# A transformer stack on one core: both halves of a tick's scores issued together in the first block

## The chip, the core and the metric

The kernel runs on one core of a Trainium2 chip. The metric is the time of one execution on the device in microseconds; lower is better. A core has a matrix engine (TensorE, in the profile PE, with its weight loads as PEld), VectorE (DVE), ScalarE (ACT), GpSimd (POOL) and SyncE (SP), which here only issues DMAs. Each engine works through its own list of instructions in the order in which the program wrote them; semaphores make one engine wait for another. TensorE writes its results into PSUM, a memory of eight banks of 128 partitions x 512 floats, and VectorE and ScalarE read them there.

## The reference, cut to what matters

A batch of 32 samples of 128 tokens x 144 channels goes through four layers in a row: an attention block with an MLP (L0), a rotation in a 64-dimensional subspace (L1), a second attention block with an MLP (L2), and an attention block with four experts of which each token uses two (L3). The change concerns the attention of L0:

```
q, k = ln(q, g_q), ln(k, g_k)                                    # 16 heads of 9 channels
attn = softmax(einsum('bhqd,bhkd->bhqk', q, k) * 9 ** -0.5)
o    = einsum('bhqk,bhkd->bhqd', attn, v)
x    = x + g_msa * (o @ w_proj + b_proj)
x    = x + g_mlp * (gelu(ln_mod(x) @ w1 + b1) @ w2 + b2)
```

For L1 the kernel also needs the Q of a QR decomposition of a 144 x 64 matrix and, for each sample, the exponential of a 64 x 64 skew matrix. Both depend on the weights and the condition alone, and the kernel computes them beside the first block.

## The kernel before, in words

**Tiling.** One sample is one tile: 128 tokens on the partitions. Four samples make a group, and some products (MLP, L2's and L3's projections) run for a group at once. The kernel is one unrolled software pipeline whose step is called a *tick*. In each tick three samples are in the attention part: `s0` gets its scores, for the maxima of the softmax; `s1`, one sample older, gets its scores again with the maxima already subtracted, for the weights; `s2`, older by one more, has its values weighed and projected. The ticks of the first block are 0 to 31, those of the second begin at tick `first[1]` = 39 (B + GAP, GAP = 7), those of the third at 71. The order of the emissions is written out by hand: the main loop (L1281 to L1325) calls the attention steps, and `fill(tick, gap)` puts whatever was planned with `put` for that place (L1168 to L1263). The program's order is each engine's order; nothing is reordered afterwards.

**A tick of the first block, in order** (L1289 to L1325). Gap "a": a QR column is broadcast (`ps_qr`, L324; ScalarE squares and copies it, GpSimd takes a root), then the transposes `ps_hT_m` of a finished sample and their two ScalarE copies hM_m and hR_m (L663). "t": two more pieces of QR on VectorE, which end in the update of `at` (L356). `scores(s0, s1, 0)`. Gap "stats": every fourth tick from tick 10 on the first part of `mlp1` (three products with `hR_m` into three banks `ps_h`, L673). `weigh(s2)`: 32 small products into `ps_o`, and ScalarE's copy `on` (L882). "b": a second linear layer `ps_f`, the values `ps_v`, the transposes `ps_hT_a`, a piece of the matrix exponential (`ps_odd`, `ps_sq` and others), the rest of that mlp1 with its three gelus. "den": the next QR column, and VectorE's statistics of the layer norms. `sums(s2)` (L889 to L894): two transposes back into `ps_o`, from which VectorE takes the reciprocals rd and spreads them to rdx. `scores(s0, s1, 1)`. "c": the projection to q and k of a later sample and its transposes (`ps_qk`, `ps_qkT`, with ScalarE's qT, kT and qksq). `divide_T` (L901), pieces of QR, `divide` (oT, L906). "d": other parts of the MLP. `largest_T` and `largest` (L808, L813): the maxima are transposed and added to q as q2, which s0's weights of the next tick need. "z": a piece of the matrix exponential, among others. `project_out`: `ps_pj` (L927), res_a (L916), and the sum into x, which GpSimd does early in the next tick.

**scores(s, w, n)** (L819) does one half of the heads. For s it fills two banks `ps_s` with four products of K = 32 and 256 columns, for w two banks `ps_w` with eight products of K = 32 and 128 columns; the rows of the two differ, so that the four 32-row parts of the array are all used. An fp32 product shows as two records in the profile. VectorE then takes the maxima of each `ps_s` bank (L854, two reductions), and ScalarE the exponentials of each `ps_w` bank (L861, two activations) into a tile `pr`.

**PSUM.** Pool `ps_o` is one bank, which `weigh`, `sums` and `divide_T` of a sample use in turn. Pool `ps_m` is the other seven, given out by `bank()` (L78). A bank goes back to the pool behind the last instruction that reads it, in the order of the program; the first product into it then waits for that reader:

```
ps_o = ctx.enter_context(tc.tile_pool(name="ps_o", bufs=1, space=PSUM))
ps_m = ctx.enter_context(tc.tile_pool(name="ps_m", bufs=7, space=PSUM))
```

Of the kernel before, what the change touches and what calls it, by code (L numbers as in the profile page):

```python
# [8 lines left out]
F32 = mybir.dt.float32  # L9
# [8 lines left out]
B, T, C = 32, 128, 144  # L18
# [47 lines left out]
def tile_kernel(ctx: ExitStack, tc: tile.TileContext, a: dict, out: bass.AP):  # L66
# [7 lines left out]
    ps_o = ctx.enter_context(tc.tile_pool(name="ps_o", bufs=1, space=PSUM))  # L74
# [3 lines left out]
    def bank(shape, name):  # L78

        n = 1  # L80
        for s in shape[1:]:
            n *= s
        t = ps_m.tile([128, 512], F32, tag="m", name=name)
        v = t[: shape[0], :n]
        if len(shape) == 3:
            v = v.rearrange("p (a b) -> p a b", b=shape[2])
        elif len(shape) == 4:
            v = v.rearrange("p (a b c) -> p a b c", b=shape[2], c=shape[3])
        return v
# [161 lines left out]
    def rows4(i):  # L251
        return slice(32 * i, 32 * i + 32)
# [44 lines left out]
    def load_gates(layer, g, n):  # L297

        t = work.tile([128, G, C], F32, tag=f"gates{n}", name=f"gates_{layer}_{g}_{n}")
        nc.sync.dma_start(  # L300
            t.rearrange("p b c -> p (b c)"),
            gates[layer, n, g * G * C : (g + 1) * G * C].partition_broadcast(128),
        )
        return t
# [315 lines left out]
    def of(s):  # L620
        layer, b = divmod(s, B)
        return layer, b, (layer, b // G), b % G
# [182 lines left out]
    def largest_T(s, ot):  # L805

        st[s]["nmT"] = bank([128, T], f"ps_nm_{s}") if ot is None else ot[:, 3 * T : 4 * T]
        nc.tensor.transpose(st[s]["nmT"], st[s].pop("nm"), ident)  # L808
# [7 lines left out]
        )  # L816
        st[s]["q2"] = q2

    def scores(s, w, n):  # L819


        mm = ([], [])
        if s is not None:
            layer, b, g, i = of(s)
            qT, kT = gr[g]["qT"], gr[g]["kT"].rearrange("p (r t) n -> p r t n", t=2)
            cols = slice(i * T, (i + 1) * T)
            ps = [bank([128, 4 * T], f"ps_s_{s}_{n}_{e}") for e in range(2)]
            if n == 0:
                st[s]["nm"] = take_nm()
            for t in range(2):  # L830
                for e in range(2):
                    rows = rows4(2 * n + e)
                    o = ps[e].rearrange("p (r t k) -> p r t k", r=2, t=2)[:, :, t, :]
                    mm[0].append((o, qT[rows, t, cols], kT[rows, :, t, cols]))
        if w is not None:
            layer, b, g, i = of(w)
            kT, q2 = gr[g]["kT"], st[w]["q2"]
            cols = slice(i * T, (i + 1) * T)
            pw = [bank([128, 4 * T], f"ps_w_{w}_{n}_{e}") for e in range(2)]
            for k in range(4):  # L840
                for e in range(2):
                    rows = rows4(2 * (1 - n) + e)
                    mm[1].append((pw[e][:, k * T : (k + 1) * T], kT[rows, k, cols], q2[rows, k % 2, :]))

        order = []
        for t in range(2):
            order += mm[0][2 * t : 2 * t + 2] + mm[1][4 * t : 4 * t + 4]
        for o, x, y in order:
            nc.tensor.matmul(o, x, y, start=True, stop=True)  # L849
        if s is not None:  # L850
            nmv = st[s]["nm"].rearrange("p (q s) -> p q s", s=SLOT)
            for e, view in enumerate(ps):
                at0 = 4 * n + 2 * e
                nc.vector.tensor_reduce(  # L854
                    nmv[:, at0 : at0 + 2, ONE : ONE + 2],
                    view.rearrange("p (r t k) -> p r t k", t=2, k=T), AX.X, ALU.max, negate=True,
                )
        if w is not None:
            pr = work.tile([128, 8, T], F32, tag="pr", name=f"pr_{w}_{n}", bufs=4)
            for e, view in enumerate(pw):  # L860
                nc.scalar.activation(  # L861
                    pr[:, 4 * e : 4 * e + 4, :].rearrange("p s q -> p (s q)"), view, AF.Exp,
                    scale=SCALE,
                )
            st[w]["pr", 1 - n] = pr

    def weigh(s):

        ot = ps_o.tile([128, 512], F32, tag="o", name=f"ps_o_{s}")
        st[s]["ot"] = ot  # L870
        po = ot[:, : 2 * T].rearrange("p (t q) -> p t q", t=2)
        v, prs = st[s].pop("v"), [st[s].pop(("pr", n)) for n in range(2)]
        for t in range(2):
            for r in range(2):
                for j in ROWS:
                    nc.tensor.matmul(  # L876
                        po[rows4(j), t, :], v[:, 4 * j + 2 * t + r, :],
                        prs[j // 2][:, 4 * (j % 2) + 2 * r + t, :],
                        start=r == 0, stop=r == 1,
                    )  # L880
        on = work.tile([128, 2, T], F32, tag="on", name=f"on_{s}")
        nc.scalar.copy(on, po)  # L882
        st[s]["on"] = on

    def sums(s):

        po = st[s]["ot"][:, : 2 * T].rearrange("p (t q) -> p t q", t=2)
        for t in range(2):
            nc.tensor.transpose(po[:, t, :], st[s]["on"][:, t, :], ident)  # L889
        den = po.rearrange("p t (s c) -> p t s c", c=SLOT)[:, :, :, ONE]  # L890
        rd = small.tile([128, 2, 8], F32, tag="rd", name=f"rd_{s}")
        nc.vector.reciprocal(rd, den)
        rdx = work.tile([128, 2, 8, SLOT], F32, tag="rdx", name=f"rdx_{s}")
        nc.vector.tensor_copy(rdx, rd.unsqueeze(3).to_broadcast([128, 2, 8, SLOT]))  # L894
        st[s]["rdx"] = rdx

    def divide_T(s):
        po = st[s]["ot"][:, : 2 * T].rearrange("p (t q) -> p t q", t=2)
        rdx = st[s].pop("rdx")
        for t in range(2):  # L900
            nc.tensor.transpose(po[:, t, :], rdx[:, t, :, :].rearrange("p s c -> p (s c)"), ident)  # L901

    def divide(s):
        po = st[s]["ot"][:, : 2 * T].rearrange("p (t q) -> p t q", t=2)
        oT = work.tile([128, 2, T], F32, tag="oT", name=f"oT_{s}")
        nc.vector.tensor_tensor(oT, st[s].pop("on"), po, ALU.mult)  # L906
        st[s]["oT"] = oT
# [254 lines left out]
    GAP = 7  # L1162
    first = (0, B + GAP, 2 * B + GAP)
# [22 lines left out]
    for layer in range(3):  # L1186
        ahead = 5 if layer == 0 else 6
        for n in range(NG):
            g = (layer, n)
            t0 = first[layer] + n * G  # L1190
            for i in range(G):
                s = layer * B + n * G + i
# [75 lines left out]
    def fill(tick, gap):  # L1268
        prepare_qr(tick, gap)
        while (tick, gap) == (last_prep, "d") and late is None:  # L1270
            prepare_qr(tick, gap)
            prepare_expm(tick, gap)

        if gap == ("t" if tick < 0 else "den" if tick < first[1] else "stats") and tick in stats:
            ln_stats(stats.pop(tick))
        for f, args in gaps.pop((tick, gap), ()):
            f(*args)
        prepare_expm(tick, gap)

    last_prep = first[1] - 8  # L1280
    for tick in range(-6, first[2] + B + 14):  # L1281
        s0, s1, s2 = (at_tick.get(tick - k) for k in range(3))
        for layer in range(3):
            for n in range(NG):
                if tick == first[layer] + n * G:
                    gr[layer, n]["ga"] = load_gates(layer, n, 0)
                if tick == first[layer] + n * G + (6 if layer else 9):
                    gr[layer, n]["gm"] = load_gates(layer, n, 1)
        fill(tick, "a")  # L1289
        while sums_later:  # L1290
            sums_later.pop()()
        fill(tick, "e")
        fill(tick, "t")
        scores(s0, s1, 0)
        fill(tick, "stats")
        if s2 is not None:
            weigh(s2)
        fill(tick, "b0")
        fill(tick, "b")
        fill(tick, "den")  # L1300
        if s2 is not None:
            sums(s2)
        fill(tick, "pre1")
        scores(s0, s1, 1)
        fill(tick, "c")
        joined = tick >= first[1]
        if s2 is not None:
            divide_T(s2)
        fill(tick, "y1")
        if s2 is not None and not joined:  # L1310
            divide(s2)
        fill(tick, "y2")
        if not joined:
            fill(tick, "d")
        if s0 is not None:
            largest_T(s0, st[s2]["ot"] if s2 is not None and joined else None)
        if s2 is not None and joined:
            divide(s2)
        if s0 is not None:
            largest(s0)  # L1320
        fill(tick, "z")
        if joined:
            fill(tick, "d")
        if s2 is not None:
            project_out(s2)  # L1325
# [167 lines left out]
```

## Time and profile before

| what | us |
| --- | --- |
| median of 3 timed runs (lowest, highest) | 1423.7 (1420.84, 1427.12) |
| the profiled execution's own time | 1412.95 |
| its span, first to last instruction | 1411.1 |
| TensorE busy in the span | 1333.3 |
| ScalarE busy | 819.2 |
| VectorE busy | 798.3 |
| GpSimd busy | 623.4 |
| first block: first scores of tick 0 to first scores of tick 31 | 40.0 to 440.7 |

The page gives each engine's busy time, then rows of 40 slices of the span in which a digit is the busy share in tenths; the row PEclk, TensorE's granted clock, is 9 in all of them. A line of the waits reads: engine and instruction, what released it, the sum of such waits in us, how often, the longest. A line of the timeline reads: start, duration, engine, line, operation, output and inputs, shapes, how many records are merged in it. TensorE's ends are modelled, so a wait inside a run of products can hide in its busy time; the starts are what to go by.

### The profile page before, as it was taken

The numbers are of one execution on the slowest core, as the hardware profiler recorded it, in microseconds if no ns is written. First come the engines' busy times: TensorE is split into PE (matmuls) and PEld (weight loads), VectorE is DVE, ScalarE is ACT, GpSimd is POOL, SyncE is SP. The second block draws the span as 40 slices with busy tenths as digits, with TensorE's granted clock in tenths as the row PEclk, the third lists the DMA queues.
The fourth block names the chain that finished last, engine by engine and source line by source line (L and its number), as shares of the span: only waits on it lengthen the run. The fifth ranks groups of instructions, "written<-read, shape, count | busy, mean of one in ns | idle before, by whom it ended". The sixth has DMA issues, their size and how long they took to land.

```text
span 1411.1 us, 36544 instructions
## 1 busy us (share of the span) xinstructions
PE 1333.3 (94%) x14530; PEld 976.5 (69%) x14530; DVE 798.3 (57%) x2652; ACT 819.2 (58%) x1912; POOL 623.4 (44%) x1647
## 2 busy tenths in 40 slices
PE   6989898999989988999999999999999999999998
PEld 4667576686766566677767666777776767677765
DVE  5798888877864256565555555544444444343211
ACT  3657767656756445666666666555555555554431
POOL 5567667654643433343333334425252525151522
PEclk9999999999999999999999999999999999999999
DMA  8200000000003100000100000200000000000000
GB/s 221 57 2 19 19 19 2 19 3 20 19 1 117 34 2 18 10 19 10 42 27 18 10 18 11 73 10 18 9 19 9 19 10 18 10 18 2 18 9 9
DMA packets 21612, 34.78 MB, mean 25 GB/s; under 512 B 2176, under 2 KB 12256, under 8 KB 21184
## 3 DMA queue, kind: packets, MB, share of 16 engines
q1 hardware_dynamic: 20848, 31.82, 7.7%
q8 instruction: 117, 1.92, 0.6%
q10 hardware_dynamic: 592, 0.59, 0.2%
q14 instruction: 55, 0.45, 0.1%
HBM read 29.93 MB, written 2.47 MB: 23 GB/s over the span
## 4 chain that ended last, share of the span: by engine, by line
PE 68%; DVE 4%; ACT 2%; issue 1%; POOL 1%; POOLq 0%; DVEq 0%
PE ps_h L673 17%; PE ps_f L953 16%; PE ps_s L849 6%; PE ps_w L849 6%; PE ps_qk L673 5%; PE ps_o L876 5%; PE ps_pj L927 3%; PE ps_v L673 2%; PE ps_o L889 1%; DVE nm L854 1%; PE ps_o L901 1%; PE ps_g L673 1%; DVE oT L906 1%; PE ps_z L985 1%; PE ps_o L808 0%
## 5 line engine op out<-in xcount | busy, mean ns | idle before, releaser
L861 ACT ACTIVATE pr<-ps_w 128x512 f32<-128x512 f32 x384 | 208.5, 596 | 165.4 <-PE ps_w L849 164.7
L854 DVE TENSOR_REDUCE nm<-ps_s 128x4 f32<-128x512 f32 x384 | 246.8, 684 | 82.3 <-PE ps_w L849 68.9
L849 PE MATMUL ps_w<-q,kT 32*128 32x128 f32 x3072 | 236.4, 284 | 0.9 <-ACT hR_m L663 0.6
L849 PE MATMUL ps_s<-kT,qT 32*128 32x256 f32 x1536 | 234.8, 408 | 0.1
L849 PEld LDWEIGHTS ps_w<-q,kT 32*128 32x128 f32 x3072 | 198.6, 187 | 16.1 <-issue 3.6
L947 ACT ACTIVATE hid<-ps_h 128x512 f32<-128x512 f32 (+1 forms) x224 | 119.2, 590 | 119.1 <-PE ps_h L673 119.1
L953 PE MATMUL ps_f<-mlps,hid 128*128 128x144 f32 x1280 | 181.2, 292 | 0.5 <-ACT hid L947 0.5
L953 PEld LDWEIGHTS ps_f<-mlps,hid 128*128 128x128 f32 x1280 | 165.1, 191 | 18.4 <-issue 11.6
L913 POOL TENSOR_TENSOR x_sb<-x_sb,res_a 128x144 f32<-128x144 f32 x96 | 47.0, 489 | 266.8 <-DVE res_a L916 266.7
L1064 DVE SCALAR_TENSOR_TENSOR acc<-ps_f,cw,acc 128x144 f32<-128x144 f32 x128 | 46.9, 367 | 197.6 <-PE ps_f L953 175.8
L849 PEld LDWEIGHTS ps_s<-kT,qT 32*128 32x128 f32 x1536 | 135.0, 186 | 26.8 <-issue 9.2
L673 PE MATMUL ps_h<-hM_m,mlps 128*128 128x512 f32 x304 | 143.8, 606 | 0.0
L876 PE MATMUL ps_o<-pr,vaug 128*32 128x128 f32 x3072 | 104.8, 277 | 0.4 <-issue 0.4
L876 PEld LDWEIGHTS ps_o<-pr,vaug 128*32 128x32 f32 x3072 | 78.7, 110 | 33.8 <-PE ps_w L849 19.0
L673 PEld LDWEIGHTS ps_h<-hM_m,mlps 128*128 128x128 f32 x304 | 53.4, 190 | 66.2 <-issue 64.7
L906 DVE TENSOR_TENSOR oT<-on,ps_o 128x256 f32<-128x256 f32 x96 | 40.0, 417 | 96.3 <-PE ps_o L808 92.9
L953 PEld LDWEIGHTS ps_f<-pair,hid 128*128 128x128 f32 x640 | 82.3, 190 | 9.6 <-issue 8.4
L953 PE MATMUL ps_f<-pair,hid 128*128 128x144 f32 x640 | 86.8, 287 | 0.2 <-ACT hid L947 0.2
L913 POOL TENSOR_TENSOR x_sb<-x_sb,res_m 128x144 f32<-128x144 f32 x64 | 32.8, 512 | 111.4 <-DVE res_m L916 111.2
L634 POOL TENSOR_SCALAR rs_m_a<-mv_m_a 128x2 f32<-128x2 f32 x81 | 15.5, 191 | 142.9 <-DVE mv_m_a L632 115.5
L663 ACT ACTIVATE hM_m<-ps_hT_m,modM 128x128 f32<-128x128 f32 x96 | 44.1, 460 | 58.4 <-PE ps_hT_m L661 58.2
L861 ACT ACT_TABLE_LOAD x55 | 70.6, 1283 | 8.4 <-PE ps_w L849 7.6
(312 smaller groups left out, 2823.2 us busy)
## 6 DMA issues: line engine op xcount, KB each, us to landing
gates<-gates SPq DMA_DIRECT2D x48, 288.0 KB, 3.6
x_sb<-in_x SPq DMA_DIRECT2D x8, 288.0 KB, 10.2
out_x<-x_sb SPq DMA_DIRECT2D x8, 288.0 KB, 2.4
mlps<-in_L_mlp SPq DMA_DIRECT2D x2, 1000.0 KB, 6.3
wt<-in_W SPq DMA_DIRECT2D x6, 320.0 KB, 8.0
pair<-in_L_mlp SPq DMA_DIRECT2D x1, 1872.0 KB, 10.1
mlps<-in_L_mlp SPq DMA_DIRECT2D x1, 1872.0 KB, 7.6
mlps<-in_L_wmod SPq DMA_DIRECT2D x4, 290.0 KB, 6.3
```

The source lines that it names most:

```text
L663: nc.scalar.activation(gr[g][f"{k}_{kind}"][:, i, :], ps[:, k == "hR", :], AF.Identity, bias=m[:, sh, b : b + 1], scale=m[:, sc, b : b + 1],)
L673: nc.tensor.matmul(ps, x, y, start=k == 0, stop=k == 1)
L849: nc.tensor.matmul(o, x, y, start=True, stop=True)
L854: nc.vector.tensor_reduce(nmv[:, at0 : at0 + 2, ONE : ONE + 2], view.rearrange("p (r t k) -> p r t k", t=2, k=T), AX.X, ALU.max, negate=True,)
L861: nc.scalar.activation(pr[:, 4 * e : 4 * e + 4, :].rearrange("p s q -> p (s q)"), view, AF.Exp, scale=SCALE,)
L876: nc.tensor.matmul(po[rows4(j), t, :], v[:, 4 * j + 2 * t + r, :], prs[j // 2][:, 4 * (j % 2) + 2 * r + t, :], start=r == 0, stop=r == 1,)
L906: nc.vector.tensor_tensor(oT, st[s].pop("on"), po, ALU.mult)
L913: nc.gpsimd.tensor_tensor(x_sb[:, b, :], x_sb[:, b, :], t, ALU.add)
L927: nc.tensor.matmul(ps, oT[:, t, :], w[:, t, :], start=t == 0, stop=t == 1)
L947: nc.scalar.activation(hid[:n, i], ps[:n], AF.Gelu_apprx_tanh)
L953: nc.tensor.matmul(ps, hid[:, at0, i, :], w2[:, m, :], start=m == 0, stop=m == NFC - 1)
L1064: nc.vector.scalar_tensor_tensor(acc, ps, w, acc, ALU.mult, ALU.add)
```

## The change

In ticks below `first[1] - GAP` = 32, thus in every tick of the first block that has an s0, the second half of the scores is issued directly behind the first. The two halves then need eight banks at once: seven of `ps_m`, and for the first bank of the first half's weights the one of `ps_o`. The second half's exponentials follow its products at once, in ScalarE's list ahead of `on` and of all of gap "b". The second half's two maxima are kept back as a function and written where the second half stood before, after `sums` and gap "pre1". Later ticks are as they were.

```diff
-    def scores(s, w, n):
+    def scores(s, w, n, at_once=False):
...
-            pw = [bank([128, 4 * T], f"ps_w_{w}_{n}_{e}") for e in range(2)]
+            pw = [
+                ps_o.tile([128, 4 * T], F32, tag="o", name=f"ps_w_{w}_{n}_{e}")
+                if at_once and n == e == 0
+                else bank([128, 4 * T], f"ps_w_{w}_{n}_{e}")
+                for e in range(2)
+            ]
...
-        if s is not None:
+
+        def maxima():
+            if s is None:
+                return
             nmv = st[s]["nm"].rearrange("p (q s) -> p q s", s=SLOT)
...
+        later = at_once and n == 1
+        if not later:
+            maxima()
         if w is not None:
             pr = work.tile([128, 8, T], F32, tag="pr", name=f"pr_{w}_{n}", bufs=4)
...
+        return maxima if later else None
...
-        scores(s0, s1, 0)
+
+        at_once = tick < first[1] - GAP
+        scores(s0, s1, 0, at_once)
+        if at_once:
+            maxima = scores(s0, s1, 1, True)
         fill(tick, "stats")
         if s2 is not None:
             weigh(s2)
...
         fill(tick, "pre1")
-        scores(s0, s1, 1)
+        if at_once:
+            maxima()
+        else:
+            scores(s0, s1, 1)
         fill(tick, "c")
```

## The prediction

> **What bounds the kernel now.** I read the page first, then the busy times by stretch of the first block, then the waits of each engine there, then the timeline of single ticks. "Tick k" is the tick that makes sample k's scores; its start is the first ps_s matmul (L849) of that tick.
>
> ```profile
> span 1411.1 us, 36544 instructions
> ...
> PE 1333.3 (94%) x14530; PEld 976.5 (69%) x14530; DVE 798.3 (57%) x2652; ACT 819.2 (58%) x1912; POOL 623.4 (44%) x1647
> ...
> DVE  5798888877864256565555555544444444343211
> ```
>
> Over the whole span PE is the full engine, but the change touches only ticks 0 to 31, from 40.0 us to about 442 us, and there (slices 2 to 12) VectorE's row stands at 7 to 8. By stretches (ticks 6 to 13, then 18 to 22):
>
> ```profile
> core 0: us, PE busy (x) PEld busy (x) DVE busy (x) ACT busy (x) POOL busy (x), PEclk, DMA share, GB/s
> ...
> 109.74:205.68 95.94, 86.68 (x1158) 67.28 (x1157) 85.72 (x310) 68.55 (x217) 67.39 (x188) 0.98 0.05 14
> ...
> 256.96:332.05 75.09, 73.88 (x1159) 57.42 (x1158) 59.71 (x210) 48.54 (x142) 39.09 (x121) 1.00 0.07 18
> ```
>
> In the first row DVE is busy 85.7 of 95.9 us in 310 instructions, so the rest is some 0.03 us between one instruction and the next: VectorE is full. In the second PE is full and VectorE is waiting. What VectorE waits for between 40 and 420 us:
>
> ```profile
> DVE rot L587 <- PE ps_sq L527: 9.3, 5, 3.7
> DVE qr L345 <- POOL qr L335: 8.1, 24, 0.7
> ...
> DVE nm L854 <- PE ps_w L849: 2.9, 4, 1.7
> ...
> DVE nm L854 <- PE ps_s L849: 1.3, 1, 1.3
> ```
>
> The maxima (nm, L854) wait only 4.2 us for scores in all. So earlier scores can give VectorE little, and later products of the rest of PE's work can cost it much. Tick 14 (start 205.68) in PE's timeline, then VectorE's, then ScalarE's:
>
> ```profile
> 206.64 1.60 PE L673 MATMUL ps_h<-hR_m,mlps 32*128 32x512 f32 x6
> 208.17 1.08 PE L876 MATMUL ps_o<-pr,vaug 128*32 128x128 f32 x32
> 209.18 2.84 PE L673 MATMUL ps_h<-hM_m,mlps 128*128 128x512 f32 x6
> ...
> 212.29 0.38 PE L889 MATMUL ps_o<-cst,on 128*128 128x128 f32 x2
> 212.60 0.48 PE L849 MATMUL ps_s<-kT,qT 32*128 32x256 f32 x2
> ```
>
> ```profile
> 206.36 0.30 DVE L916 TENSOR_TENSOR res_a<-ps_pj,gates 128x144 f32<-128x144 f32 x1
> ...
> 209.28 1.28 DVE L854 TENSOR_REDUCE nm<-ps_s 128x4 f32<-128x512 f32 x2
> ...
> 213.13 0.24 DVE L892 RECIPROCAL rd<-ps_o 128x16 f32<-128x16 f32 x1
> 213.41 0.29 DVE L894 COPY rdx<-rd 128x256 f32<-128x256 f32 x1
> 213.76 1.29 DVE L854 TENSOR_REDUCE nm<-ps_s 128x4 f32<-128x512 f32 x2
> ```
>
> ```profile
> 206.60 0.47 ACT L663 ACTIVATE hR_m<-ps_hT_m,modR 128x128 f32<-128x128 f32 x1
> 206.96 1.09 ACT L861 ACTIVATE pr<-ps_w 128x512 f32<-128x512 f32 x2
> ```
>
> The reader should see that the first maxima end at 210.56, 4.9 us after the tick's start, because VectorE is still at the last tick's work; that sums (L889) end only 0.46 us before VectorE takes rd; and that rd is followed at once by the second maxima, now and in the changed program.
>
> **The change, part by part.**
>
> *VectorE's order.* The second maxima are written after sums and "pre1" either way, so VectorE's list is the same, instruction for instruction. Gain and loss come only through its waits. No DMA is moved; SP's and POOL's lists are unchanged too.
>
> *PE's order.* The second half's 12 products (24 records) move ahead of mlp1's first part, weigh, gap "b", the QR broadcast of "den" and sums. A half takes 1.10 us from its first start to the next work's (tick 14: 212.60 to 213.71); inside it the four groups start 0.22 us apart, the lead-in and run-out being the rest. Joined without a wait, 8 groups take about 1.98 instead of 2.20 us: -0.2 us a tick, worth something only where PE is the bound (some 10 ticks: -2 us).
>
> *Banks of the second half.* It takes the last four of the seven: in program order those of the expm piece of "z", of ps_pj, of ps_qr and of ps_hT_m. They come free with res_a (L916, VectorE; 0.0 to 1.9 us after the tick's start) and hR_m (L663, ScalarE; 1.34 to 1.55 us, tick 14: 207.07, so 1.39). The first half is through at 1.0, so the fourth product waits about 0.4 us, and the pair ends near 2.5 instead of 2.2: +0.3. In ticks 19 to 23 the old first half already lost 0.7 us to ps_qr's bank (start to weigh 1.8 instead of 1.1), which now falls to the second half; there it is -0.4.
>
> *What follows on PE* starts about 1.1 to 1.4 us later, counted from the tick's start: weigh at 2.5 instead of 1.1. In ticks whose exponentials first load ScalarE's table (1283 ns, L861) weigh also waits for the exponential that frees ps_o, as that bank now carries the first weights: ready near 3.2 us. PE has this work back at the place where scores stood before, after sums. So PE loses only its waits, while VectorE gets PE's products of "b", "den" and sums 1.1 us later or more.
>
> *Who has cover.* I compared, tick by tick, the end of sums with the start of rd. Ticks 3, 9, 11, 12, 15, 16, 17 and 19 have 2.4 to 3.9 us between: nothing is lost, as PE stood there anyway for the QR column (L324 waited 1.1, 1.6 and 2.1 us for `at` in ticks 3, 11, 15) or for rdx. Ticks 5 and 8 have 0.3 us: +0.7 each. Ticks 6 and 7: 1.4, so +0.3 each. Ticks 13, 20, 21, 23: VectorE waits in "b" for PE itself (ps_even, ps_sq); the products come 0.7 to 1.4 later, but PE has its later work closer: +0.8, +1.0, +0.3, +0.3. Ticks 25 and 28: +0.4 and +1.2. Ticks 0, 30, 31, where maxima waited for scores or PE is full to the end: -0.7 together. Sum 4.6, less 0.6 for the exponentials that no longer stand before qT, kT and qksq: **about +4 us**.
>
> *The five mlp1 ticks (10, 14, 18, 22, 26)* take three banks directly behind the second half. Free in program order are then those of the first maxima, of one first exponential and of the second exponentials. No row shows which are taken, so I bound it. If ScalarE's: ready 2.4, 3.1, 3.7, weigh starts near 4.5. If the first maxima's: in tick 14 at 4.2 and 4.9; the two later products need another 1.0, so weigh starts at 6.0. Behind it, from weigh's start to that of sums, stand 1.05 + 3.06 us of PE work in this tick (from the rows above), so sums start at 8.6 or 10.1 instead of 6.61, and rd comes at 9.0 or 10.5 instead of 7.45: +1.5 or +3.0 on a full VectorE. The same for ticks 10, 18, 22, 26 with their own maxima (ends 5.2, 4.4, 4.2, 4.4): +0.4 to +2.2, +1.1 to +2.1, +0.6 to +1.7, +1.5 to +2.5. Together +5 to +11.5. I take 10, near the upper end: the banks of the maxima are given back first in program order, and in the trace of before the next product after a half (ps_hT_a, tick 18: 263.20) is issued after them. Below nothing this can't go: the products moved ahead take PE's time first.
>
> **A rule against the change.** The row first: in tick 14 maxima hold two banks till 210.56, and the change lets two more be held from about 208 until past rd and rdx. The Trainium skill's page "PSUM — Partial Sum Buffer", section "Summary: rules for kernel authors", says to empty PSUM promptly because it is small ("Evacuate promptly — 2 MiB is tight"). By the rule alone every one of 31 ticks pays: the first work after weigh (ready at 3.6) needs a bank of the first maxima (4.2 to 5.3), some 0.7 us a tick or 22 us. By the rows, most of these waits fall where PE waited for VectorE anyway; I count 4 for them. The rows decide, the rule sets my upper end.
>
> **Sum.** +4 + 10 = +14 us. The profiled execution took 1412.95 us (span 1411.1 and 1.85 around it), so it becomes 1427; that is 10.8 under the median 1423.7 of the timed runs, and moved by 14 this becomes **1438**. About 0.5% (7.1 us) is what a measurement can tell from no change.
>
> **The rivals.**
>
> *Hidden by VectorE (chance 0.21), 1427.* Only the lower end for mlp1 holds (+5), the +4 is taken up by slack that I don't see, and the seam gives its -2: +3. For it: VectorE's list is the same and full in 250 us. Against it: in ticks 10, 14 and 26 rd follows sums within 0.5 us.
>
> *Faster (0.07), 1415.* The mechanism is the seam with scores early: maxima no longer wait for scores (4.2), the seam saves 0.2 in ten PE-bound ticks (2), qkv's wait for qksq after mlp1 ticks goes (three times 0.5; tick 15: 0.47 at 218.12): -8 to -9. It decides if the second half follows within 2.05 us of the tick's start and mlp1's first products don't wait. Against it: hR_m ends at 1.34 or later in every tick of ps_hT_m.
>
> *Starved of banks (0.17), 1450.* mlp1 pays 11.5 and every other tick pays for the maxima's banks where it has no cover, 13 to 15 more: +26. This is also the case in which the change does not do what it says, since the halves then don't run together.
>
> **Chances.** The forecast has 0.55; its own range is 1430 to 1446. Leaving out under 0.1 below and 0.1 above, the range is 1424 to 1452. Slower by over 0.5%: 0.55 + 0.17 and a little of the hidden case's neighbourhood: 0.73. Within: 0.21. Faster: 0.06.
>
> **What would show it.** In the changed profile: (1) ps_s of both halves within 2.7 us of each tick's start, with a wait for hR_m or res_a inside the second; (2) in ticks 10, 14, 18, 22, 26 a PE wait of 1 to 2.5 us before ps_h or weigh, named DVE nm (if ACT pr: the lower end); (3) rd's wait for ps_o (L889) in the first block grown from 1.4 us to some 10, the maxima's wait for ps_s and ps_w gone; (4) VectorE's and PE's busy sums unchanged, the block longer by 14, everything after it as long as before. I am wrong if (2) is absent, or if VectorE makes the lateness up inside the tick.

## The result, and the profile after

The changed kernel takes 1455.1 us (median of 4 runs, 1448.9 to 1456.2) beside 1424.4 us of the kernel before: 1.0245 times as long, with an interval of 1.0205 to 1.0284. The forecast was 1438, at most 1452. The sign was right; the loss is 31 us where 14 were forecast.

In the page of the changed kernel the busy sums are those of before within 0.4%, so no work was added. The span is 36 us longer, and VectorE's row in slices 2 to 12 reads 6 to 8, where it read 6 to 9 before.

```profile
span 1447.2 us, 36528 instructions
...
PE 1338.7 (93%) x14530; PEld 980.2 (68%) x14530; DVE 798.9 (55%) x2652; ACT 819.4 (57%) x1912; POOL 624.2 (43%) x1647
...
DVE  5788788776774336565556555544443444344211
```

Laid side by side from one tick's first ps_s to the next, ticks 0 to 32 take 38.7 us more; everything behind them takes 1.2 us less. (In this count tick 31 runs on to the second block's first scores, and tick 32 is the first tick of that block.) The five mlp1 ticks take 17.6 of it, the other ticks 21.1. VectorE's waits from tick 0 to tick 30, first before, then after (sum, times, longest), name the places:

```profile
DVE rot L587 <- PE ps_sq L527: 9.3, 5, 3.7
...
DVE odd_lo L564 <- PE ps_odd L527: 2.6, 1, 2.6
DVE res_m L916 <- PE ps_f L953: 2.4, 2, 1.2
...
DVE rd L892 <- PE ps_o L889: 0.3, 1, 0.3
```

```profile
DVE rot L587 <- PE ps_sq L527: 13.6, 5, 6.6
DVE res_m L930 <- PE ps_f L967: 13.5, 11, 1.6
DVE rd L906 <- PE ps_o L903: 12.3, 7, 5.7
...
DVE odd_lo L564 <- PE ps_odd L527: 7.2, 1, 7.2
```

So VectorE stands for TensorE's products in three places: the sums, as was forecast (8.8 of the 12.3 us in the mlp1 ticks 10 and 14); the matrix exponential's products ps_odd and ps_sq, whose longest waits of 7.2 and 6.6 us are in the mlp1 ticks 18 and 22; and ps_f, mlp2's product, to which the forecast gave no cost. TensorE's own waits in the same ticks of the changed kernel:

```profile
PE ps_h L673 <- DVE nm L864: 7.6, 5, 2.0
PE ps_o L890 <- ACT pr L874: 6.7, 9, 0.8
...
PE ps_v L694 <- DVE nm L864: 2.0, 2, 1.5
PE ps_f L967 <- DVE nm L864: 1.7, 3, 1.1
PE ps_hT_a L660 <- DVE nm L864: 1.5, 4, 0.8
```

Four of these five lines are waits for the first maxima, thus for their banks: 7.6 us in the five mlp1 ticks, and 5.2 us in nine other places. Before, none of the four stood among TensorE's waits. The second line is the weighing, which waits for the exponential whose bank it now shares.

### The profile page after: what moved, and what is told of

The parts are those of the page before. It is cut to its first block, busy times and chain, and to the rows that moved or that the text cites. A ratio compares the mean times of both kernels' runs of the same rounds, so it can differ in the third digit from the quotient of the medians.

```text
span 1447.2 us, 36528 instructions
## 1 busy us (share of the span) xinstructions
PE 1338.7 (93%) x14530; PEld 980.2 (68%) x14530; DVE 798.9 (55%) x2652; ACT 819.4 (57%) x1912; POOL 624.2 (43%) x1647
## 4 chain that ended last, share of the span: by engine, by line
PE 66%; DVE 4%; ACT 2%; issue 1%; POOL 1%; POOLq 0%; DVEq 0%; ACTq 0%
PE ps_h L673 17%; PE ps_f L967 15%; PE ps_s L856 6%; PE ps_w L856 6%; PE ps_qk L673 5%; PE ps_o L890 5%; PE ps_pj L941 3%; PE ps_v L673 2%; PE ps_o L903 1%; DVE nm L864 1%; PE ps_o L915 1%; ACT pr L874 1%; PE ps_g L673 1%; DVE oT L920 1%; PE ps_z L999 1%
## 5 line engine op out<-in xcount | busy, mean ns | idle before, releaser
L856 PE MATMUL ps_w<-q,kT 32*128 32x128 f32 x3072 | 233.5, 285 | 0.9 <-ACT hR_m L663 0.6
L856 PE MATMUL ps_s<-kT,qT 32*128 32x256 f32 x1536 | 230.0, 409 | 0.0
L856 PEld LDWEIGHTS ps_w<-q,kT 32*128 32x128 f32 x3072 | 199.0, 189 | 17.6 <-ACT hR_m L663 6.6
L967 PEld LDWEIGHTS ps_f<-mlps,hid 128*128 128x128 f32 x1280 | 164.0, 190 | 20.7 <-issue 10.8
L634 POOL TENSOR_SCALAR rs_m_a<-mv_m_a 128x2 f32<-128x2 f32 x81 | 15.5, 192 | 143.5 <-DVE mv_m_a L632 116.1
L874 ACT ACT_TABLE_LOAD x55 | 70.6, 1283 | 8.4 <-PE ps_w L856 7.6
```

Source lines behind the costliest of these rows:

```text
L874: nc.scalar.activation(pr[:, 4 * e : 4 * e + 4, :].rearrange("p s q -> p (s q)"), view, AF.Exp, scale=SCALE,)
L967: nc.tensor.matmul(ps, hid[:, at0, i, :], w2[:, m, :], start=m == 0, stop=m == NFC - 1)
```

## The experiments

The theories that the expectations name: A, TensorE's products come later for VectorE, and mlp1's first products stand for the banks of the first maxima. B, a loss is handed on from tick to tick. C, an idle TensorE loses clock. D, the second maxima hold their banks too long. E, the bank shared with the weighing. F, the second half's own products ahead of everything. H, the first maxima's banks also hold up the ticks without mlp1. "Chip's before" is the kernel before, run between the others of a group. Tick lengths are compared with those of the profile of before.

### Where: the five ticks, the others, the maxima (chip's before 1418.7)

```diff
-        at_once = tick < first[1] - GAP
+        at_once = tick in (10, 14, 18, 22, 26)
```

> The halves stand together only in the five ticks that hold mlp1's first part (10, 14, 18, 22, 26). Theory A (VectorE waits for PE products that come later; in these ticks mlp1's first products also wait for the banks of the first maxima): these five ticks are longer by 17 to 18 us in all, as in the changed kernel (17.6), the others as before; kernel 1440 to 1443. Theory B (each tick with joined halves hands its lateness to the next, so the five are dear only after others): under 10 us, 1434 or less. Theory C (most of the loss is TensorE's lower clock after its waits): about 3.5 us above the sum of the waits alone, in ticks 10 and 18 only.

Measured: 1441.0 us, 1.0132 (1.0059 to 1.0204), with single runs from 1429.6 to 1450.9. In its profile the five ticks take 24.2 us more, and ticks 5 to 8, 12, 13, 16, 17, 19 to 21 and 23 to 25 are those of before within 0.15 us: B falls. But four of the five have half clock, which is why they exceed A's 17 to 18 us, and tick 0, where nothing was changed, takes 9.3 us more.

```diff
-        at_once = tick < first[1] - GAP
+        at_once = tick < first[1] - GAP and tick not in (10, 14, 18, 22, 26)
```

> The complement: halves together in every tick of the first block but 10, 14, 18, 22, 26. Theory A: +17 to +21 us over the kernel before (the rest of the changed kernel's +35 to +38), 1441 to 1445, with ticks 12, 16, 17, 20, 24, 25 each longer by about 1.0 to 1.4 because VectorE waits for ps_f before res_m. Theory B: more than half of it gone, under +9. Theory C: the half clock seen in ticks 23, 28, 29 and 31 goes with the waits, so it stays here.

Measured: 1432.4 us, 1.0098 (1.0070 to 1.0127). The other ticks take 21.3 us more, at full clock each as in the changed kernel, but for 11 and 15, which are no longer shorter; the five take 0.9. The median, 13.7 us over its kernel before, lies under the 1441 to 1445 that A named.

```diff
-            maxima = scores(s0, s1, 1, True)
+            scores(s0, s1, 1, True)()
...
-        if at_once:
-            maxima()
-        else:
+        if not at_once:
             scores(s0, s1, 1)
```

> The changed kernel with the second half's maxima read at once, behind the first half's, instead of behind sums. Theory A: little is repaired, as PE's order and the banks of the first maxima stay; VectorE does 1.2 us of maxima while it would wait anyway, so some of its waits in gap b are filled: -5 to -12 us against the changed kernel, still 1443 or more. Theory D (the two banks held until behind sums starve what follows): back to within 5 us of the kernel before, 1430 or less. A cost is possible too: in ticks where VectorE is full, res_m, qkn and the statistics come 1.2 us later, and with them PE's later work.

Measured: 1449.0 us, 1.0214 (1.0189 to 1.0239). Giving the second maxima's banks back at once repairs next to nothing: D falls.

### How: order and bank apart

The second half behind gap "b" (chip's before 1418.7):

```diff
-        if at_once:
-            maxima = scores(s0, s1, 1, True)
         fill(tick, "stats")
...
         fill(tick, "b")
+        if at_once:
+            maxima = scores(s0, s1, 1, True)
         fill(tick, "den")
```

> The changed kernel with the second half issued behind gap b, ahead of den's QR column and of sums; its maxima still behind sums. Theory A: weigh, mlp1's first part and all of b are on time again, only the QR column and sums come 1.1 us later; the loss falls from 31-35 us to 2 to 8 (ticks 5, 8, 10, 14, 26 without cover for sums), 1427 to 1433. Theory D (held banks): the two banks are held for as little as before, so it can't tell there. Theory E (ps_o shared with the first weights is the cost, as weigh waits for the exponential): weigh still waits for it, some 0.7 us in every fourth tick; then 6 us or more stay.

Measured: 1446.3 us, 1.0187 (1.0143 to 1.0231): missed. Some ticks are repaired (17: +0.0, 19: +0.1), but the profile records 80 us of half clock in ticks 0 to 32 where the kernel before has 15 and the changed one 32. Ticks 12, 16, 20, 24 and 28, in which ScalarE loads a table, keep their loss, and tick 0, at half clock for 15.5 us, takes 6.6 us more. (The 64.9 us that an expectation below names for this run leave out the stretch from 30.7 to 54.6 us.)

The bank alone, with before's order (chip's before 1421.4):

```diff
-            pw = [bank([128, 4 * T], f"ps_w_{w}_{n}_{e}") for e in range(2)]
+            pw = [
+                ps_o.tile([128, 4 * T], F32, tag="o", name=f"ps_w_{w}_{n}_{e}")
+                if n == e == 0 and w < B - 1
+                else bank([128, 4 * T], f"ps_w_{w}_{n}_{e}")
+                for e in range(2)
+            ]
```

> The kernel before, with only the bank of the first weights' first tile taken from the weighing's two banks, nothing else changed and no order moved. Theory E (sharing the weighing's banks makes it wait for the exponential, and that is part of the loss): weighing later by 0.5 to 1 us a tick, +5 to +15 us, 1424 to 1434. Theories A and C: the exponential of the first tile is done 1.1 us into the tick or less, and the weighing needs it anyway: 1416 to 1422, not to be told from the kernel before.

Measured: 1432.1 us, 1.0079 (1.0051 to 1.0106): E's side, +10.7. The expectation was wrong in its ground: it said that the weighing needs that exponential anyway, but it uses the exponentials of the tick before. (It also speaks of the weighing's two banks; ps_o has one.) Sharing the bank ties it to this tick's:

```profile
PE ps_o L881 <- ACT pr L866: 23.8, 23, 2.2
```

A plain tick at full clock loses up to 0.9 us by it. Tick 0's +9.3 us in this profile is not the bank's: e1 and e16, which leave that tick as it was, have the same. Ticks 12, 16, 20, 24 and 28, in which ScalarE loads a table ahead of the first exponential (1283 ns, in the changed kernel's page too), have the weighing at 3.3 us from their start instead of 1.1 to 1.8 and lose 2.0 to 3.5, all five with some half clock. In the changed kernel the weighing also stands for a late exponential in ticks 11, 15, 19, 23, 27 and 31, where a table load has come to stand ahead of it.

The order alone: e4 with every weights' bank from the pool of seven (chip's before 1417.8):

```diff
             pw = [
-                ps_o.tile([128, 4 * T], F32, tag="o", name=f"ps_w_{w}_{n}_{e}")
-                if at_once and n == e == 0
-                else bank([128, 4 * T], f"ps_w_{w}_{n}_{e}")
+                bank([128, 4 * T], f"ps_w_{w}_{n}_{e}")
                 for e in range(2)
             ]
```

> The order of the kernel with the second half behind gap b (products of the second half ahead of the sums, its maxima still behind the reciprocals), but with every weights' bank from the pool of seven, so that the weighing shares its bank with nothing, as before the change. Theory E+A (two parts: the shared bank alone gave +10.7 us, the order alone gives the rest at the rate of ticks 5 to 8 and 14, some 0.5 to 2 us where the sums are what VectorE needs next, about nothing elsewhere): weighing at 1.1 us again in the plain ticks, +5 to +12 us over the kernel before of the same chip, 1425 to 1433. Rival A alone (the order carries nearly everything, the bank is a trifle): +17 to +27.

Measured: 1430.0 us (13 runs), 12.2 us over its kernel before by the medians, 1.0079 (1.0051 to 1.0107), as E and A together say. The tables' ticks 12, 16 and 20 are back at -0.1, +0.1 and -0.2.

The same pool with the second half behind the weighing:

```diff
-        if at_once:
-            maxima = scores(s0, s1, 1, True)
         fill(tick, "stats")
         if s2 is not None:
             weigh(s2)
+        if at_once:
+            maxima = scores(s0, s1, 1, True)
         fill(tick, "b0")
```

> The second half's products right behind the weighing instead of ahead of mlp1's first part, again with no bank shared with the weighing: the second half's last tile takes the bank of a first maximum, read 3 to 4 us into a tick. Theory E+A: weighing at 1.1 us in the plain ticks, TensorE waits up to 1 us for nm in the second half, sums later by 1.6 to 2.5 us as in the changed kernel but mlp1's first part not held up: +10 to +18 us, 1430 to 1438. Rival A alone: as the changed kernel, +28 to +36.

Measured: 1462.1 us, 1.0309 (1.0252 to 1.0366): missed, the slowest but one. With seven banks the second half itself stands for a bank of the first maxima, by 1 us on average and up to 2.2, and everything behind it too:

```profile
PE ps_w L851 <- DVE nm L859: 17.2, 18, 2.2
```

### The banks of the first maxima

mlp1's first products behind the weighing (chip's before 1421.4):

```diff
-put2(t0 + 10, "stats", "b", mlp1, g, 0, (0, 1, 2), True)
+put2(t0 + 10, "b0", "b", mlp1, g, 0, (0, 1, 2), True)
```

> The changed kernel with mlp1's first products (those that take the banks of the first maxima and of an exponential) moved behind the weighing in ticks 10, 14, 18, 22 and 26; nothing else moved. Theory A (TensorE stands at mlp1's first products for those banks, with the weighing queued behind): the waits of ps_h for nm (7.6 us in five) go below 1.5 us, weighing at 2.5 to 3.3 us from a tick's start, the five ticks together fall from +17.6 to between +5 and +10, median 1443 to 1449. Rival F (the second half's 1.6 us of products ahead of everything, not the banks, costs these ticks): they stay above +13, median 1451 to 1456.

Measured: 1441.7 us, 1.0167 (1.0126 to 1.0208). The five ticks come to +8.3, and their wait to

```profile
PE ps_h L673 <- DVE nm L864: 1.5, 4, 0.7
```

so 5 of their 13 us at full clock were the wait for the banks, and F alone, which said above +13, falls. But 8.3 us stay: the second half's products ahead of everything have their share.

The first maxima earlier, in the changed kernel and in the kernel before (chip's before 1421.3):

```diff
-                pieces = {"a": 1, "t": 2, "den": 1, "y1": 1, "y2": 1}
+                pieces = {"a": 1, "stats": 2, "den": 1, "y1": 1, "y2": 1}
```

> The changed kernel with the two QR pieces of gap t (some 2.5 us of VectorE's work, ahead of the first maxima) moved to gap stats, so that VectorE takes the first maxima first and their two banks come back 2 to 2.5 us earlier; the QR column for TensorE comes 1.3 us later. Theory H (in the ticks without mlp1, too, the first product behind the weighing waits for a bank of the first maxima, and VectorE then waits for that product): TensorE's waits for nm ahead of ps_h, ps_v, ps_f and ps_hT_a (12.8 us together) fall below 5, ticks 12, 16 and 17 (+1.0, +1.3, +1.1) come to +0.3 or less against the same move made in the kernel before; difference to that kernel +15 to +24 instead of +31 to +35. Rival (only the later issue counts, the banks are a trifle there): ticks 12, 16, 17 keep +1, and the difference stays at +28 to +36.

> The kernel before with the same move of the two QR pieces behind the first maxima, as the base for the run above. VectorE's work is the same; TensorE already waited 8.6 us for the QR column in 15 places, and that comes about 1.3 us later in some 17 ticks: +3 to +15 us over the kernel before, 1421 to 1433. If the maxima's lateness had been a bound of its own: 1412 to 1418.

Measured: 1431.6 us, 1.0120 (1.0065 to 1.0174), and for the base 1417.4 us, 0.9976 (0.9954 to 0.9998), not slower by 3 us or more as was expected. By the medians the change now costs 14.2 us and not 31; by the ratios some 20 and not 35, with about 8 us to either side for the 20. So about half of the loss is gone. What is left of TensorE's waits for nm and pr in e13:

```profile
PE ps_nm L808 <- DVE nm L864: 9.3, 14, 1.1
...
PE ps_o L890 <- ACT pr L874: 5.9, 8, 0.8
```

The waits of ps_h, ps_v, ps_f and ps_hT_a for nm (12.8 us) are gone, and against the base the five mlp1 ticks take 3.5 us more, where they took 13.4 at full clock. Outside mlp1 the move repairs less: 17 ticks are at full clock in all four profiles, and they take 9.4 us more than the base where the changed kernel took 12.7. H holds for ticks 1, 2 and 17 (0.0, 0.0 and +0.4 against the base) and in part for 6 and 7 (+0.2 of 0.6), but missed for 12 and 16 (+1.3 and +1.7, said to be +0.3 or less), and ticks 5, 8 and 20 keep their +1.1, +1.1 and +1.2 too.

### The clock

Idle transposes in the wait of the five ticks (chip's before 1421.4):

```diff
+        if tick in (10, 14, 18, 22, 26):
+            ot = out_bank(s2)
+            for _ in range(8):
+                nc.tensor.transpose(ot[:, 2 * T : 3 * T], ident, ident)
         fill(tick, "stats")
```

> The changed kernel, with eight idle transposes (128x128, into columns of the weighing bank that nothing reads) on TensorE ahead of mlp1's first products in ticks 10, 14, 18, 22 and 26, where TensorE waited 1.2 to 2.0 us for the first maxima's banks; the result is the same. Eight such transposes take about 1.0 us (0.11 to 0.12 us apiece in a row), so none of them lengthens those waits by more than a few tenths. Theory C (an idle TensorE in these ticks lets the granted clock fall to 0.50 for the next 3.4 us or more, and that is about 2.3 us each of ticks 10's and 18's loss): no half clock in these five ticks, ticks 10 and 18 fall from +4.7 and +4.6 to about +2.4, median 1448 to 1452. Theory A alone (only the waits count, the half clock falls where it may): the five ticks stay at +17 to +18, median 1453 to 1457.

Measured: 1449.4 us, 1.0212 (1.0179 to 1.0246). The five take 13.2 instead of 17.6 us more, tick 10 +1.8 and tick 18 +3.0, and none of them falls to half clock behind its wait. In sum little is won: half clock falls elsewhere, 39 us of it in ticks 0 to 32, the span is 1446.7 us where the changed kernel's is 1447.2, and the two ratios' intervals overlap. The same with six of them ahead of every weighing in e4:

```diff
         if s2 is not None:
+            if at_once:
+                ot = out_bank(s2)
+                for _ in range(6):
+                    nc.tensor.transpose(ot[:, 2 * T : 3 * T], ident, ident)
             weigh(s2)
```

> As the kernel with the second half issued behind gap b (1446.3 us, half clock for 64.9 us of its first 600), with six idle transposes on TensorE ahead of the weighing in every tick of the block, where TensorE waited about 1.0 us for the exponentials in 23 ticks; the result is the same. Theory C: half clock inside ticks 0 to 32 falls below 25 us, and what is left is the waits: ticks 5, 6, 7, 8, 14, 20, 25, 26 together +9 and the rest near 0: median 1428 to 1436. Rival (the clock follows something else, or the idle transposes cost what they save): 1443 to 1452.

Measured: 1466.4 us, 1.0303 (1.0248 to 1.0358): missed. The transposes go to the weighing's bank, so they stood for the same exponential as the weighing and came behind the wait instead of into it (24.5 us in 23 places, now at their line). This run says nothing for or against C, only that the filling must not need what is waited for.

The changed kernel once more:

> The changed kernel once more, nothing edited. Theory C (the clock is granted by stretches of 3.41 us whose grid does not follow the kernel, and a stretch in which TensorE was busy for less than about 0.6 is followed by half clock; so the same wait is punished in one execution and not in the next): half clock falls at other places than ticks 10, 18, 23, 28 and 31 alone, ticks 10 and 18 differ from +4.7 and +4.6 by more than 1 us in at least one of the two, while ticks at full clock agree within 0.1 us. Rival (the half clock belongs to what these ticks do): the same ticks, the same lengths.

Measured: 1456.9 us, a single run. Half clock now falls in ticks 14, 18, 22 (twice 3.4 us) and 26, no longer in 10: the five take +2.0, +4.4, +4.7, +6.2 and +4.1 us where they took +4.7, +2.8, +4.6, +3.0 and +2.5. From tick 5 on the other ticks, where both are at full clock, agree within 0.15 us. The records of the granted clock change on a grid of 3.41 us. Here are the grid's stretches around tick 14's wait for the maxima, in the first profile of the changed kernel and then in this one (from:to, length, then busy time of PE, PEld, DVE, ACT and POOL, granted clock, DMA share, GB/s):

```profile
214.28:217.69 3.41, 2.59 (x49) 2.15 (x48) 2.73 (x13) 3.14 (x11) 2.79 (x9) 1.00 0.28 100
217.69:221.10 3.41, 2.49 (x38) 1.40 (x38) 3.38 (x8) 0.30 (x1) 1.92 (x5) 1.00 0.26 78
221.10:224.52 3.42, 3.42 (x24) 1.76 (x13) 0.63 (x4) 3.08 (x6) 0.72 (x3) 1.00 0.00 0
```

```profile
217.30:220.70 3.40, 1.67 (x10) 0.61 (x10) 3.22 (x11) 1.09 (x2) 1.76 (x7) 1.00 0.45 140
220.70:224.10 3.40, 3.40 (x36) 2.20 (x35) 1.45 (x5) 1.40 (x2) 1.51 (x4) 0.50 0.00 0
```

The work and the wait (1.74 us named in both timelines) are the same. In the first execution the grid cuts the wait in two, so that TensorE is busy for 2.59 and 2.49 of 3.41 us, and the clock stays; in the second one stretch holds the whole wait, 1.67 of 3.40 us are busy, and 0.50 follows. C holds in this pair: the same wait is followed by half clock or not, by where the grid lies.

### The ticks that became shorter

```diff
-        at_once = tick < first[1] - GAP
+        at_once = tick in (0, 11, 15, 27)
```

> Both halves together only in ticks 0, 11, 15 and 27, which were shorter by 0.5 to 0.9 us in the changed kernel and in most of the others, and before's order in all other ticks. Theory A (a tick's gain and loss is its own): those four ticks together -2.5 us, the rest unchanged, 0.1 to 0.2% below the kernel before, inside what the measurement can tell. Theory C adds that the granted clock may fall in another place, up or down by some us. If the gain was bought by the lengthening of the tick ahead (10, 14, 26 are the ones ahead of 11, 15 and 27): no gain, or a loss of up to 2 us.

Measured: 1412.0 us (22 runs) beside 1417.8: 0.9950 (0.9931 to 0.9968), half a per cent below the kernel before, and by more than those ticks' own 1.3 us. Split, with `tick == 0` and `tick in (11, 15, 27)` (chip's before 1421.3):

> Both halves together in tick 0 alone. If that tick gives the gain of the four (-5.8 us by the medians, of which the ticks of one profile show 1.6): 1411 to 1414 beside a kernel before of about 1418. If it gives only its own 0.6 us: 1416 to 1419.

> Both halves together in ticks 11, 15 and 27 alone. By their own lengths in the four-tick kernel (0.0, 0.0 and -0.7, with ticks 28 and 29 -0.3 and -0.4 behind them): -1 to -1.5 us, 1416 to 1418 beside a kernel before of about 1418. If the gain of the four is theirs: 1411 to 1414.

Measured: tick 0 alone 1414.0 us, 0.9966 (0.9942 to 0.9990); the three 1421.1 us, 1.0020 (0.9990 to 1.0050). At full clock tick 27 keeps its -0.7 us, but 11 and 15 gain 0.1 or less: in the changed kernel their gain came with the longer ticks ahead of them. The gain is tick 0's, and it is clock. Tick 0's first 14 us, without the change there (e16) and with it (e15):

```profile
40.00:47.00 7.00, 7.00 (x32) 6.16 (x31) 4.19 (x16) 2.00 (x10) 3.85 (x14) 0.50 0.00 0
47.00:54.00 7.00, 7.00 (x90) 5.04 (x90) 1.64 (x8) 1.21 (x6) 1.84 (x5) 0.50 0.02 5
```

```profile
40.00:47.00 7.00, 7.00 (x123) 6.10 (x122) 4.92 (x21) 3.06 (x13) 3.37 (x12) 1.00 0.00 0
47.00:54.00 7.00, 6.70 (x76) 4.19 (x75) 5.60 (x26) 5.59 (x19) 4.77 (x16) 1.00 0.28 78
```

In the 11 profiles with both halves together in tick 0 it takes 10.5 to 11.3 us. In the eight in which the second half stays behind gap "b" or the sums it takes 16.8 to 21.1 us seven times, and once 11.8: that once is the profile of before. Why the clock comes back sooner with the halves together is not shown.

Tick 0 together with the earlier maxima of e14 (chip's before 1421.8):

> Both halves together in tick 0 alone, and the two QR pieces behind the first maxima in all ticks: the two moves that each came out a little below the kernel before (-0.34% and -0.24%). Tick 0 at full clock (10.5 to 11.2 us long instead of 17 to 21), the other ticks as in the run with the QR move alone: the two add up, -0.4 to -0.7%, 1410 to 1415 beside a kernel before of 1418 to 1421. If both gains came from the same half-clock stretch: no better than tick 0 alone, -0.2 to -0.4%.

Measured: 1412.7 us (22 runs), 0.9942 (0.9927 to 0.9958). This is the best ratio here, but it can't be told from e11's or from tick 0 alone.

## Why the prediction was wrong, step by step

**VectorE's list, PE's order, the signs: right.** VectorE's work is the same (798.9 us). Sign (1) showed: the second half follows at 1.0 us (at 1.7 to 1.9 in ticks 4, 24 and 29, which have half clock), and its last product starts at 1.7 to 2.8, in tick 29 at 3.4. Sign (2) showed: ps_h waits for nm in all five ticks, 7.6 us. Sign (3) did in its first part: rd's wait grew to 12.3 us, from 0.3 up to tick 30 (1.4 was named); the maxima's waits for scores fell only from 6.9 to 2.4 us. Of sign (4) the busy sums held and the rest stayed as it was; the block is longer by 39 and not 14.

**The mlp1 ticks: mechanism and upper end right, two sizes low.** ps_h took the first maxima's banks. Tick 14 with the times that the forecast gave its upper end (weighing 6.0, sums 10.1, rd 10.5 from the start at 214.26):

```profile
218.61 1.73 PE L673 MATMUL ps_h<-hR_m,mlps 32*128 32x512 f32 x6 [1.74 <-DVE nm L864]
220.26 1.08 PE L890 MATMUL ps_o<-pr,vaug 128*32 128x128 f32 x32
...
224.38 0.38 PE L903 MATMUL ps_o<-cst,on 128*128 128x128 f32 x2
```

```profile
224.87 0.26 DVE L906 RECIPROCAL rd<-ps_o 128x16 f32<-128x16 f32 x1 [3.07 <-PE ps_o L903]
```

That is 6.00, 10.12 and 10.61. At full clock the five take +2.0, +2.8, +3.0, +3.0 and +2.5 (tick 18 from e5, the only profile of the whole change that has it at full clock), 13.4 against 10 taken and 11.5 at most. (Before's tick 10 has 3.4 us of half clock; against that tick at full clock in e15 or e16 its loss is 3.0 and the sum 14.3.) Ticks 18 and 22 exceed their upper ends of +2.1 and +1.7: their weighing came 3 us later and sums and rd moved by the same 3 us, as there was no slack.

**"Who has cover", +4: this step failed, and it cost most.** With as little half clock as these profiles have, the ticks outside mlp1 take about +17.5 (each tick's shorter length of the two profiles of the changed kernel, 28 and 31 from e7 and e5). The step's own terms add up to 5.3 and not to 4.6, so it should have read +4.7; that is the small part. The large one: I looked for cover between the end of sums and rd, and in four ticks at ps_even and ps_sq. VectorE also takes res_m from ps_f, well ahead of rd, and there was none. Tick 17, "nothing is lost": before, ps_f was through early,

```profile
245.92 1.49 PE L953 MATMUL ps_f<-mlps,hid 128*128 128x144 f32 x10
```

```profile
249.14 0.30 DVE L916 TENSOR_TENSOR res_m<-ps_f,gates 128x144 f32<-128x144 f32 x1
```

and after, ps_f stands for a bank of the first maxima, and res_m for ps_f:

```profile
260.87 1.49 PE L967 MATMUL ps_f<-mlps,hid 128*128 128x144 f32 x10 [1.13 <-DVE nm L864]
```

```profile
262.40 0.31 DVE L930 TENSOR_TENSOR res_m<-ps_f,gates 128x144 f32<-128x144 f32 x1 [0.99 <-PE ps_f L967]
```

The 0.99 us come back in the tick's +1.1. In tick 17 the delay is a bank's. In ticks 13, 16, 20 and 21 ps_f has no such wait in front of it and comes late because the weighing ahead of it does; res_m waits 1.0 to 1.6 us there. Where no ps_f stands in the tick, VectorE waits at the sums, and they come later than the 1.1 us that was forecast. Tick 5, before and after:

```profile
100.11 1.08 PE L876 MATMUL ps_o<-pr,vaug 128*32 128x128 f32 x32
...
103.91 0.38 PE L889 MATMUL ps_o<-cst,on 128*128 128x128 f32 x2
```

```profile
100.48 1.08 PE L890 MATMUL ps_o<-pr,vaug 128*32 128x128 f32 x32
...
104.43 0.38 PE L903 MATMUL ps_o<-cst,on 128*128 128x128 f32 x2
```

```profile
104.92 0.26 DVE L906 RECIPROCAL rd<-ps_o 128x16 f32<-128x16 f32 x1 [1.23 <-PE ps_o L903]
```

Counted from the tick's start (99.00 and 97.88) the weighing comes at 2.60 instead of 1.10, without a wait in front of it, and the sums at 6.55 instead of 4.91: 1.6 us later with 0.4 us of cover. The eight ticks that were said to be covered take +2.9, with 9 as forecast, 11 and 15 even shorter by 0.5, 19 longer by 0.7, and 12, 16 and 17 by 1.0 to 1.3. Ticks 5 to 8 take +3.5 (2.0 forecast), 13, 20, 21 and 23 +4.1 (2.4), 25 and 28 +2.8 (1.6), 0, 30 and 31 +1.3 (-0.7). Ticks 1, 2, 4, 24, 27 and 29, which the list left out, take +2.9.

**The rule against the change: near in number, by luck.** From the Trainium skill's page "PSUM — Partial Sum Buffer", section "Summary: rules for kernel authors", I had put some 0.7 us on each of 31 ticks, which is 18 us for the 26 outside mlp1, and by my reading of the rows 4. They paid 17.5. But the wait that this estimate rests on is there in few ticks: outside mlp1, TensorE stands for the first maxima's banks in nine places, 5.2 us in all and 0.5 us or more only in ticks 1, 3, 9 and 17; and e13, which removes these waits, leaves 9.4 of 12.7 us. Most of the loss is plain lateness. In ticks 5 to 9, 13, 17, 21 and 25 the weighing starts at 2.5 to 2.7 us behind the second half's products, without a wait; in ticks 12, 16 and 20 it starts at 3.4, of which 0.75 us are the wait for the exponential that shares its bank. The forecast had both times right (2.5 and 3.2) and gave them too small a price. e9, which has the second half behind these products and shares no bank, has the weighing back at 1.1 to 2.0 us in these ticks and takes -0.2 to +0.6 us more in each of them. The place alone is enough in some: e4, which does share the bank, has +0.5, 0.0 and 0.0 in ticks 13, 17 and 21.

**The clock: not in the sum.** By these shortest lengths the ticks take 13.4 + 17.5 = 31 us more; the profile has 39. I put the difference of 8 down to half clock: the profile records 32 us of it in ticks 0 to 32, against 15 before, and 17 us more at half speed are some 8 us lost, by estimate.

**Profile to median: the offset was not constant.** I carried 10.8 us from before's profile over to the forecast. Before's profile was the one of eight in which such a tick 0 ran almost wholly at full clock; the others were 5 to 9 us longer there. The changed kernel's tick 0 has no such loss, and its profiled execution lies 6.2 us below its median. Summed over these steps: 1438 + 13.5 (cover) + 3.4 (mlp1) + 8 (clock) - 4.6 (offset) - 1.2 (behind the block) - 1.5 (tick 0 starts 1.5 us earlier) = 1455.6. The sum closes by its making, as every term but the first is measured; it shows the sizes and not the causes.

**The rivals.** "Starved of banks" (1450, chance 0.17) was 5 us short. It named the right place for mlp1; in the other ticks the banks are the smaller part, and the halves did run together, which it denied. "Hidden by VectorE" and "faster" fail by the 12.3 and 13.5 us that VectorE waits.

**Open.** How the loss of 31 us by the medians divides between waits and clock is known only for profiled executions. e8's 10.7 and e9's 12.2 us don't add up to it, but neither has the change's first place for the second half, and both carry their own half clock. No run keeps that place without the shared bank, so the share of the bank in the changed kernel itself is not measured. And why some stretches with the same busy share are followed by half clock and others not stays open.

## What to carry to other kernels

Cover is to be counted for every product that a full engine takes in the stretch, in the order of its list, and not only for the one at the end of the chain that is moved. Where a change holds all banks of a pool, the next tile to be allocated waits for the reader that is last to empty its bank: moving that reader forward (e13, 14 us left by the medians) brought back more than moving mlp1's first products (e7, 20 left) or the second half with its shared bank (e4, 28 left). Moving the second half and sharing no bank (e9) left 12. And before an offset between one profile and a median is carried over, one should ask which tick of that profile had luck with the clock.

## What the runs showed of the hardware that was not expected

The granted clock changes between 1.00 and 0.50 in steps of 3.41 us, on a grid whose place against the kernel differs from execution to execution. The records of all nineteen profiles, over the first 600 us, give these counts of stretches at full clock that were followed by half clock, by the share of the stretch in which TensorE was busy:

| busy share | stretches | followed by half clock |
| --- | --- | --- |
| under 0.47 | 60 | 59 |
| 0.47 to 0.60 | 123 | 51 |
| 0.60 to 0.75 | 335 | 22 |
| 0.75 to 0.85 | 331 | 4 |
| over 0.85 | 2039 | 9, each the first stretch that its profile records |

Of the stretches at half clock, 1 of 44 that were busy for less than 0.88 was followed by full clock, and 132 of 157 that were busy throughout. The Trainium skill's "TensorE: Matmul & The Clock Gate" ("What's actually happening") gives the same free-running window, 3413 ns. Its section "HAM oscillation — how this bites in real kernels" puts the danger at idle gaps above some 3.4 us; here waits of 1.2 and 1.7 us (ticks 22 and 14 of e12) were enough. Behind tick 22's wait of 1.16 us in e12 the weighing took 1.94 instead of 1.08 us. So the price of a wait in one profile is not its price in the next, and single ticks should be compared over two profiles before a loss is put down to the order of the work.
